# A three-layer feature-interaction kernel: the first pair of blocks read from two half tables

## The chip, the cores and the metric

The kernel runs on one core of a Trainium2 chip, in float32. The metric is the device time of a launch in microseconds (us); the time before is 734.22 us, the median of 3 runs (733.21 to 736.08). "Profile" and "trace" mean the record of one further execution by the hardware profiler. The engines are TensorE (PE, matrix multiplication; PEld is its weight load), VectorE (DVE), ScalarE (ACT), GpSimd (POOL) and SyncE (SP). GpSimd, ScalarE and SyncE issue transfers (DMA).

## What is computed

A batch of 1024 rows x has 39 fields of 64 numbers each. Three layers multiply every field of the layer's input with every field of x and mix the products by weights; each layer's output is summed over the 64 numbers, and a last row of weights makes one number per batch row:

```python
def _cin_layer(Xk, X0, W, b):
    O = W.shape[0]
    Hk, Fdim = (Xk.shape[1], X0.shape[1])
    Wr = W.reshape(O, Hk, Fdim)
    return jnp.einsum('bhe,bfe,ohf->boe', Xk, X0, Wr) + b[None, :, None]
X0 = sparse_embedding
Xk = X0
outs = []
for W, b in ((W0, b0), (W1, b1), (W2, b2)):
    Xk = _cin_layer(Xk, X0, W, b)
    outs.append(Xk.sum(axis=-1))
cin_output = jnp.concatenate(outs, axis=-1)
return cin_output @ fc_w.T + fc_b
```

Only sums of the second and third layer are wanted, so the kernel folds their weights with the last row (`v2` and its products), and the big work is one multiplication by 128 columns of weights: 64 for the first layer's output and 64 for the folded rest. It runs over the products of two fields; a product of fields a and b and that of b and a are the same, so their weights are added first and each pair is multiplied once.

## The kernel before

**Blocks and steps.** The batch is cut into 32 blocks of 32 rows (`BLK` = 2048 columns, a column being one of 64 numbers of one row). A block's x lies in memory field by field, 39 rows of 2048 columns and a row of ones, in one of three tables `xd`; a table holds a pair of blocks, n and n + 1, in rows 0 to 39 and 40 to 79. From it five tiles r (128 partitions x 2048) are gathered, each a chosen list of 128 fields (`lists`, an index per partition), so that the products of six pairs of tiles (`PAIRS`: 0·1, 0·2, 3·1, 3·2, 0·4, 3·4) hold nearly every pair of fields. What is missing is in a seventh product, u·v, shared by a pair of blocks: u and v have 4 groups of 32 partitions, one for each half (1024 columns, `SUB`) of each of the two blocks.

**Order of a pair of blocks.** Steps (n, 0) to (n, 5), then (n, 6), the u·v step, then (n + 1, 0) to (n + 1, 5). In each step VectorE multiplies two r tiles into p (`product`, L219; u·v L221) and TensorE multiplies p by the weights `wa`, a quarter of 512 columns at a time, into four banks of a block (`multiply`, L559). The u·v step (`join`, L579 and L590) uses 32-row pieces of TensorE and writes the banks of both blocks. There are four buffers p, and VectorE is asked for step k + 4 when TensorE is told of step k. After a block's last step ScalarE and VectorE multiply the two halves of its result and sum over the 64 numbers (`finish`, L607, L609, L620), and ScalarE copies 39 fields (`fields`, L602). On VectorE `finish` of a block stands between the products that are four steps ahead: that of block 0 between (1, 3) and (1, 4).

**Gathers and loads.** GpSimd issues all gathers (`gather_rows`, L174) in program order: `roll(n)` makes the five r tiles of a block, `roll_small(n)` u and v of a pair. `load(n)` (L168) brings a block's x into its table; most are issued by SyncE, those of blocks 1, 4 and 5 by GpSimd. A gather waits for the load of its table, for the last reader of its tile, and for the eighth DMA of GpSimd before it, as eight semaphores go round. Waits are put in by the framework from what each instruction reads and writes; the order is that of the program, written by hand.

**The first pair.** To start early, block 0's x is loaded by ScalarE in two halves `xh` of 1024 columns, and tiles 0 to 3 are gathered from these by halves (L389 to L394), with `load(1)` between. SyncE copies both halves into table 0 (L396), since tile 4 of block 0 (it needs the row of ones), u and v, and block 1's tiles are gathered from that table. During this TensorE folds the weights (L406 to L487), and VectorE adds weights for each step (`weight_rows`, L526), which TensorE transposes (`weight_turn`, L543). `spin` (L279) multiplies ones, to no use but keeping TensorE going. The loop at L689 to L730 then runs the steps; a step's `product` of number 5 of a block is followed by the `roll` of the block two later.

Of the kernel before, what the change touches and what calls it, by code (L numbers as in the profile page):

```python
# [62 lines left out]
FT = F + 1  # L63
# [84 lines left out]
def cin_kernel(ctx: ExitStack, tc: tile.TileContext, x, w0t, b0, w1, b1, w2, b2, fc_w, fc_b, out):  # L148
# [9 lines left out]

    xv = x.rearrange("b f e -> f b e")
    xd = [dram.tile([2 * FT, BLK], F32, name=f"xd{k}") for k in range(NTAB)]  # L160
    xh = [dram.tile([F, SUB], F32, name=f"xh{k}") for k in range(2)]

    def bank(name):
        return psum.tile([128, MM], F32, name=name, tag="po")
# [1 line left out]
    def load(n, engine=nc.sync):  # L166
        first = n % 2 * FT
        engine.dma_start(  # L168
            xd[n // 2 % NTAB][first : first + F].rearrange("f (b e) -> f b e", e=E),
            xv[:, n * BB : (n + 1) * BB, :],  # L170
        )

    def gather_rows(dst, table, k):
        nc.gpsimd.indirect_dma_start(  # L174
            dst, None, table, bass.IndirectOffsetOnAxis(ap=lists[:, k : k + 1], axis=0)
        )

    def roll(n, tiles=range(NT)):
        for i in tiles:
            k = n % 2 * NT + i  # L180
            gather_rows(rt[n % 2][:, i], xd[n // 2 % NTAB][: FT if k < NT else 2 * FT], k)

    def roll_small(n):
        table = xd[n // 2 % NTAB].rearrange("f (t c) -> (f t) c", c=SUB)
        for k, dst in enumerate((ut, vt)):
            gather_rows(dst[n // 2 % 2], table, 2 * NT + k)

    wa = const.tile([128, NCHUNK, 3 * H], F32, name="wa")
    columns = const.tile([128, 3], F32, name="columns")
# [8 lines left out]
    wfin = const.tile([H + F, 1], F32, name="wfin")  # L198
    kfin = const.tile([NY * 32, 1], F32, name="kfin")

    lists = const.tile([128, 2 * NT + 2], I32, name="lists")
# [23 lines left out]
    with prep as prep:  # L225
# [24 lines left out]
        nc.sync.dma_start(fcrow, fc_w)  # L250
        def load_half(k):
            nc.scalar.dma_start(
                xh[k].rearrange("f (b e) -> b f e", e=E), x[k * SB : (k + 1) * SB]
            )

        nc.scalar.dma_start(w2s, w2.rearrange("o (s n) -> (o s) n", s=2))
# [30 lines left out]
        spin()  # L287


        tmp = prep.tile([128, 16], F32, name="tmp")  # L290
# [77 lines left out]
        def fill_ones(k, engine, src):  # L368
            engine.dma_start(xd[k][F::FT].rearrange("r (p c) -> p r c", c=128), src)

        fill_ones(0, nc.gpsimd, ones)


        nc.vector.tensor_scalar(unit, apart, 0, None, ALU.is_equal)
        for h in (0, H):
# [4 lines left out]
        r, most, seat, far = (new() for _ in range(4))  # L380
# [6 lines left out]
        nc.vector.tensor_scalar(most, r, 23.0, 2.0, ALU.min, ALU.mult)  # L387

        halves = [slice(0, SUB), slice(SUB, BLK)]  # L389
        for k, cols in enumerate(halves):  # L390
            for i in range(4):
                gather_rows(rt[0][:, i, cols], xh[k], i)
                if k and i == 1:
                    load(1, nc.gpsimd)  # L394
        for k in (1, 0):
            nc.sync.dma_start(xd[0][0:F, halves[k]], xh[k])  # L396
        roll(0, (4,))

# [29 lines left out]
            )  # L428
        nc.vector.tensor_tensor(steps_at, steps_at, steps_by, ALU.mult)
        fused(seat, row, 96.0, seat, ALU.is_ge, ALU.add)  # L430
        step(row, 64.0, 2.0 * FT - 1.0, far)
        nc.vector.tensor_reduce(jumps, steps_at, AX.X, ALU.add)
        fused(most, r, 4.0, most, ALU.add, ALU.add)
        column = blocks.rearrange("h k (f j) -> h (k f) j", j=32)[:, :, 0]
# [26 lines left out]
        for k, n in enumerate((8, 5)):  # L461
            for t in range(2):
# [104 lines left out]
    def join(n, p):  # L567
        open_block(n + 1)

        def tiles(t, side):  # L570
            rows = slice(SQUARE * t, SQUARE * t + SQUARE)
            return rows, po[n + t // 2][2 * t % 4 + side]

        for side in range(2):
            for t in range(4):
                for half in range(2):
                    rows, dst = tiles(t, side)
                    at = (side + half) * H
                    nc.tensor.matmul(  # L579
                        dst[half * H : half * H + H],  # L580
                        wa[rows, NPAIR, at : at + H],
                        p[rows, bass.ts(side, MM)],
                        start=t >= 2,
                        stop=t < 2 and half == side,
                    )
        for t in range(4):
            for side in range(2):
                rows, dst = tiles(t, side)
                half = (1 - side) * H
                nc.tensor.matmul(  # L590
                    dst[half : half + H],
                    wa[rows, NPAIR + 1, H : 2 * H],
                    ut[n // 2 % 2][rows, bass.ts(side, MM)],
                    start=False,
                    stop=t < 2,
                )

    def fields(n):
# [88 lines left out]
        multiply(n, c, p[n, c], (1,))  # L687

    for at, (n, c) in enumerate(steps[:-TAIL]):  # L689
        if c == 0 and 2 <= n and n + 4 < NBLK:  # L690
            load(n + 4)
        quarters = range(BLK // MM)
        if at < 3:
            quarters = quarters[2:]
        if at < NPAIR and at > 1:
            multiply(n, c, p[n, c], quarters[:1])
            weight_turn(steps[at + 1][1])
            quarters = quarters[1:]
            if at == NPAIR - 1:
                multiply(n, c, p[n, c], quarters[:2])  # L700
                weight_turn(NPAIR + 1)
                quarters = quarters[2:]
        if c == NPAIR:
            join(n, p.pop((n, c)))
        else:
            multiply(n, c, p.pop((n, c)), quarters)
        if not at:
            fields(0)
            nc.scalar.copy(ones1, ones)
            fill_ones(1, nc.sync, ones1)  # L710
            for k in (2, 3):
                load(k)
        if at == NPAIR - 2:
            weight_rows(NPAIR + 1)
            for k in (NPAIR, NPAIR + 1):
                spread(k)
        if at - 1 in over:
            finish(over[at - 1])
            fields(over[at - 1] + 1)
        if at + AHEAD < len(steps):  # L720
            n, c = steps[at + AHEAD]
            if at + AHEAD <= NPAIR:
# [83 lines left out]
```

## Time and profile before

| | |
|---|---|
| time, median of 3 runs | 734.22 us (733.21 to 736.08) |
| time of the profiled execution | 733.14 us |
| its span, first to last instruction | 731.4 us |
| TensorE busy | 724.7 us, 99% of the span |
| VectorE busy | 638.3 us, 87% |
| GpSimd busy | 397.6 us, 54% |
| chain that ended last | TensorE 99% |
| L559, 128x512 multiplications | 1536 records, mean 594 ns |
| L219, products | 198, mean 2224 ns |
| L174, gathers into r from the tables `xd` | 156, mean 1938 ns |
| L174, gathers into r from the halves `xh` | 8, mean 996 ns |
| bytes moved by DMA | 197.24 MB, mean 270 GB/s |

Busy time is the share of the span in which an engine executes; overlapping instructions count once. A line of a timeline reads: start in us from the span's start, us taken, engine, line, operation, output tile and inputs, number of instructions merged into it, and in brackets the idle time of that engine before it and what ended it. A line of the chain reads: start, us, engine, output, line. In the lines on stretches, after the stretch and the busy times stand TensorE's granted clock, DMA's busy share and GB/s. One 32-bit multiplication shows as two records.

### The profile page before, as it was taken

What the parts mean: (1) busy time and instruction counts of PE and PEld (TensorE: products, weight loads), DVE (VectorE), ACT (ScalarE), POOL (GpSimd) and SP (SyncE); (2) the same over time, 40 slices, a digit from 0 to 9 for tenths busy, and PEclk for the clock granted to TensorE, in tenths of its full rate; (3) what the DMA queues carried; (4) which work ended last, traced back from release to release, by engine and by line L of the source; (5) the groups of instructions that cost most, each with busy time, mean ns of one, the idle gap of its engine ahead of it and who ended that gap; (6) DMA issues with size and microseconds to landing.
All of it is one profiled execution on the core that took longest, in us unless ns stands there. A gap on an engine that the chain in (4) does not pass through costs nothing.

```text
span 731.4 us, 6351 instructions
## 1 busy us (share of the span) xinstructions
PE 724.7 (99%) x2375; PEld 316.1 (43%) x2375; DVE 638.3 (87%) x521; ACT 166.9 (23%) x240; POOL 397.6 (54%) x254
## 2 busy tenths in 40 slices
PE   8999999999999999999999999999999999999998
PEld 4444444444444444444444444444444444444443
DVE  6999798988889988889988889888898988889885
ACT  3332121222212222221222212222121221212222
POOL 6789886536555445754537555455654547545300
PEclk9999999999999999999999999999999999999999
DMA  8997899789575887757679675896767777565700
GB/s 268 376 337 280 315 342 356 290 307 338 232 273 231 281 336 286 270 225 285 269 288 330 223 289 219 304 348 236 268 256 274 301 287 266 224 252 236 288 0 0
DMA packets 65983, 197.24 MB, mean 270 GB/s; under 512 B 40110, under 2 KB 40179, under 8 KB 45984
## 3 DMA queue, kind: packets, MB, share of 16 engines
q0 software_dynamic: 28784, 185.56, 65.5%
q1 hardware_dynamic: 35468, 9.29, 5.5%
q10 hardware_dynamic: 1700, 1.99, 1.0%
q8 instruction: 18, 0.29, 0.1%
q14 instruction: 13, 0.11, 0.0%
HBM read 196.76 MB, written 10.60 MB: 284 GB/s over the span
## 4 chain that ended last, share of the span: by engine, by line
PE 99%; DVE 0%; DMA 0%; issue 0%; ACT 0%; DVEq 0%
PE po L559 91%; PE po L579 4%; PE po L590 2%; PE idle L279 0%; PE pv L406 0%; PE pt L487 0%; PE small L323 0%; PE pv L487 0%; PE pw L418 0%; DMA fcrow<-in_fc_w 0%; PE tr L543 0%; DVE g L609 0%; DVE pairs L526 0%; DVE sums L631 0%; ACT z L607 0%
## 5 line engine op out<-in xcount | busy, mean ns | idle before, releaser
L559 PE MATMUL po<-p,wa 128*128 128x512 f32 x1536 | 666.0, 594 | 0.0
L219 DVE TENSOR_TENSOR p<-r 128x2048 f32<-128x2048 f32 (+2 forms) x198 | 434.1, 2224 | 72.4 <-PE po L559 67.1
L559 PEld LDWEIGHTS po<-p,wa 128*128 128x128 f32 x1536 | 290.5, 190 | 371.7 <-issue 354.6
L174 POOL DMA_INDIRECT r<-xd,lists x156 | 302.3, 1938 | 267.1 <-issue 266.2
L607 ACT ACTIVATE z<-po,columns 64x512 f32<-64x512 f32 x128 | 87.3, 682 | 380.1 <-PE po L590 217.9
L609 DVE SCALAR_TENSOR_TENSOR g<-po,b0s,z 64x512 f32<-64x512 f32 x128 | 95.9, 749 | 9.3 <-ACT z L607 5.3
L602 ACT COPY g<-r 39x1024 f32<-39x1024 f32 x64 | 66.7, 1043 | 155.0 <-DVE sums L620 126.8
L620 DVE TENSOR_REDUCE sums<-g 103x16 f32<-103x1024 f32 x62 | 75.6, 1220 | 2.1
L174 POOL DMA_INDIRECT u<-xd,lists x16 | 38.9, 2432 | 7.5 <-issue 4.6
L174 POOL DMA_INDIRECT v<-xd,lists x16 | 38.5, 2403 | 4.9 <-issue 4.9
L579 PE MATMUL po<-p,wa 32*64 32x512 f32 x512 | 31.6, 600 | 0.0
L221 DVE TENSOR_TENSOR p<-u,v 128x1024 f32<-128x1024 f32 x16 | 19.5, 1218 | 0.0
L579 PEld LDWEIGHTS po<-p,wa 32*64 32x64 f32 x512 | 9.4, 131 | 20.2 <-issue 19.4
L590 PE MATMUL po<-u,wa 32*64 32x512 f32 x256 | 17.0, 587 | 0.0
L174 POOL DMA_INDIRECT r<-xh,lists x8 | 8.0, 996 | 4.8 <-DVE tmp L387 2.7
L590 PEld LDWEIGHTS po<-u,wa 32*64 32x64 f32 x256 | 5.7, 132 | 8.0 <-issue 8.0
L526 DVE TENSOR_TENSOR pairs<-both 128x2 f32<-128x2 f32 (+27 forms) x59 | 6.1, 171 | 0.2
L544 ACT COPY wa<-tr 128x128 f32<-128x128 f32 x8 | 2.1, 266 | 16.2 <-PE tr L543 16.2
L279 PE MATMUL idle<-const-float32-1.0 128*128 128x256 f32 (+1 forms) x8 | 4.0, 596 | 0.8 <-PEq L793 0.8
L543 PE MATMUL tr<-unit,pairs 128*128 128x128 f32 x8 | 2.4, 294 | 2.2 <-DVE pairs L526 2.2
L543 PEld LDWEIGHTS tr<-unit,pairs 128*128 128x128 f32 x8 | 1.2, 151 | 4.7 <-ACT pairs L524 2.7
L168 POOL DMA_DIRECT2D xd<-in_x x3 | 3.2, 1055 | 0.0
(97 smaller groups left out, 56.7 us busy)
## 6 DMA issues: line engine op xcount, KB each, us to landing
xd<-in_x SPq DMA_DIRECT2D x28, 312.0 KB
r<-xd,lists POOLq DMA_INDIRECT x156, 8.9
xd<-in_x POOLq DMA_DIRECT2D x3, 312.0 KB, 7.6
w2s<-in_w ACTq DMA_DIRECT2D x1, 624.0 KB
w1s<-in_w ACTq DMA_DIRECT2D x1, 624.0 KB
w0s<-in_w0t ACTq DMA_DIRECT2D x1, 380.2 KB
xh<-in_x ACTq DMA_DIRECT2D x2, 156.0 KB
xd<-xh SPq DMA_DIRECT2D x2, 156.0 KB
```

The lines of the kernel that those rows point to most:

```text
L174: nc.gpsimd.indirect_dma_start(dst, None, table, bass.IndirectOffsetOnAxis(ap=lists[:, k : k + 1], axis=0))
L219: nc.vector.tensor_tensor(p[:, cols], r[:, i, cols], r[:, k, cols], ALU.mult)
L221: nc.vector.tensor_tensor(p[:, 0:SUB], ut[n // 2 % 2], vt[n // 2 % 2], ALU.mult)
L279: nc.tensor.matmul(idle[:, 0:cols], nc.const_aps.tensor(1.0, (128, 128), F32), nc.const_aps.tensor(1.0, (128, cols), F32), start=True, sto ...
L526: nc.vector.tensor_tensor(out, diagonal(a, b, sa, sb), diagonal(b, a, sb, sa), ALU.add)
L559: nc.tensor.matmul(po[n][m], wa[:, c, side : side + 2 * H], p[:, bass.ts(m, MM)], start=n % 2 == 0 and c == 0, stop=n % 2 == 1 and c == NP ...
L579: nc.tensor.matmul(dst[half * H : half * H + H], wa[rows, NPAIR, at : at + H], p[rows, bass.ts(side, MM)], start=t >= 2, stop=t < 2 and ha ...
L590: nc.tensor.matmul(dst[half : half + H], wa[rows, NPAIR + 1, H : 2 * H], ut[n // 2 % 2][rows, bass.ts(side, MM)], start=False, stop=t < 2,)
L602: nc.scalar.copy(gt[H : H + F], rt[n % 2][0:F, 0, bass.ts(m, SUB)])
L607: nc.scalar.activation(z[one], po[n][m][other], AF.Identity, bias=fc0s[other])
L609: return lambda: nc.vector.scalar_tensor_tensor(g[n][m // 2][0:H, at], po[n][m][one], b0s[one], z[one], ALU.add, ALU.mult)
L620: nc.vector.tensor_reduce(sums[:, b_at : b_at + SB], g[n][m // 2].rearrange("p (b e) -> p b e", e=E), AX.X, ALU.add,)
```

## The change

- The halves `xh` become tables of 80 rows each, like `xd` but with 1024 columns: rows 0 to 38 block 0's x, row 39 ones, rows 40 to 78 block 1's x, row 79 ones. The ones are written by two DMAs of GpSimd.
- All gathers of the first pair read these: tiles 0 to 3 of block 0 as before, tile 4 in two halves, u and v in two halves of 64 partitions each, block 1's five tiles in two halves each.
- SyncE's copies into table 0 are dropped. Block 1's x is loaded in two halves by GpSimd, after the eight gathers of tiles 0 to 3 instead of between them.
- The groups of u and v change places, so that the first 64 partitions belong to the first half of the columns; `seat`, `far` and `lists` follow (two more columns of `lists` for the halves), and so do the banks in `join`.
- Table 0 is first used for block 6; its row of ones is written later. The loads of blocks 6 and 7 are issued by GpSimd instead of SyncE.
- The name of the change also speaks of no filling on TensorE between T and the first turn. The diff has no such edit: the calls of `spin` are the same in both kernels.

```diff
-    xh = [dram.tile([F, SUB], F32, name=f"xh{k}") for k in range(2)]
+    xh = [dram.tile([2 * FT, SUB], F32, name=f"xh{k}") for k in range(2)]
...
     def gather_rows(dst, table, k):
+        at = lists[0 : dst.shape[0], k : k + 1]
         nc.gpsimd.indirect_dma_start(
-            dst, None, table, bass.IndirectOffsetOnAxis(ap=lists[:, k : k + 1], axis=0)
+            dst, None, table, bass.IndirectOffsetOnAxis(ap=at, axis=0)
+        )
+
+    def roll_half(n, i, h):
+        k = n * NT + i
+        rows = F if n == 0 and i < NT - 1 else (n + 1) * FT
+        gather_rows(rt[n][:, i, bass.ts(h, SUB)], xh[h][0:rows], k)
...
     def roll_small(n):
-        table = xd[n // 2 % NTAB].rearrange("f (t c) -> (f t) c", c=SUB)
         for k, dst in enumerate((ut, vt)):
-            gather_rows(dst[n // 2 % 2], table, 2 * NT + k)
+            if n:
+                table = xd[n // 2 % NTAB].rearrange("f (t c) -> (f t) c", c=SUB)
+                gather_rows(dst[n // 2 % 2], table, 2 * NT + k)
+            else:
+                for h in range(2):
+                    gather_rows(dst[0][h * H : h * H + H], xh[h], 2 * NT + 2 + k)
...
-        fill_ones(0, nc.gpsimd, ones)
-
+        for k in range(2):
+            nc.gpsimd.dma_start(
+                xh[k][F::FT].rearrange("r (p c) -> p r c", c=128), ones[0:8]
+            )
...
-        for k, cols in enumerate(halves):
-            for i in range(4):
-                gather_rows(rt[0][:, i, cols], xh[k], i)
-                if k and i == 1:
-                    load(1, nc.gpsimd)
-        for k in (1, 0):
-            nc.sync.dma_start(xd[0][0:F, halves[k]], xh[k])
-        roll(0, (4,))
+        for at in range(8):
+            roll_half(0, at % 4, at // 4)
+        for k in range(2):
+            nc.gpsimd.dma_start(
+                xh[k][FT : FT + F].rearrange("f (b e) -> f b e", e=E),
+                xv[:, BB + k * SB : BB + (k + 1) * SB, :],
+            )
+        for k in range(2):
+            roll_half(0, 4, k)
...
-        step(row, 64.0, 2.0 * FT - 1.0, far)
+        step(row, 64.0, 1.0 - 2.0 * FT, far)
...
-        nc.vector.tensor_tensor(seat, seat, far, ALU.add)
+        nc.vector.tensor_scalar(half_seat, seat, float(FT), None, ALU.mult)
+        fused(seat, seat, 2.0 * FT, far, ALU.mult, ALU.add)
...
-        nc.vector.tensor_scalar(lists[:, 2 * NT :], both_of, 2.0, seat, ALU.mult, ALU.add)
+        nc.vector.tensor_scalar(lists[:, 2 * NT + 2 :], both_of, half_seat, None, ALU.add)
+        nc.vector.tensor_scalar(
+            lists[:, 2 * NT : 2 * NT + 2], both_of, 2.0, seat, ALU.mult, ALU.add
+        )
         roll_small(0)
-        roll(1)
+        for i in range(NT):
+            for k in range(2):
+                roll_half(1, i, k)
...
-        fill_ones(2, nc.gpsimd, ones)
+        for k in (2, 0):
+            fill_ones(k, nc.gpsimd, ones)
...
-            return rows, po[n + t // 2][2 * t % 4 + side]
+            return rows, po[n + t % 2][t // 2 * 2 + side]
...
-        if c == 0 and 2 <= n and n + 4 < NBLK:
+        if c == 0 and 4 <= n and n + 4 < NBLK:
             load(n + 4)
...
-                if n < 2:
+                if n < 4:
                     load(n + 4, nc.gpsimd)
```

More of the change, by code (lines that the diff above doesn't have):

```diff
@@ L199, in cin_kernel @@
     kfin = const.tile([NY * 32, 1], F32, name="kfin")
-    lists = const.tile([128, 2 * NT + 2], I32, name="lists")
+    lists = const.tile([128, 2 * NT + 4], I32, name="lists")
     rt = [const.tile([128, NT, BLK], F32, name=f"r{k}") for k in range(2)]
@@ L252, in load_half @@
             nc.scalar.dma_start(
-                xh[k].rearrange("f (b e) -> b f e", e=E), x[k * SB : (k + 1) * SB]
+                xh[k][0:F].rearrange("f (b e) -> b f e", e=E), x[k * SB : (k + 1) * SB]
             )
@@ L287, in cin_kernel @@
         spin()
-        tmp = prep.tile([128, 16], F32, name="tmp")
+        tmp = prep.tile([128, 18], F32, name="tmp")
         wide = prep.tile([128, 5, NT], F32, name="wide")
@@ L379, in cin_kernel @@
             )
-        r, most, seat, far = (new() for _ in range(4))
+        r, most, seat, far, half_seat = (new() for _ in range(5))
         both_of = prep.tile([128, 2], F32, name="both_of")
@@ L582, in join @@
                         p[rows, bass.ts(side, MM)],
-                        start=t >= 2,
-                        stop=t < 2 and half == side,
+                        start=t % 2 == 1,
+                        stop=t % 2 == 0 and half == side,
                     )
@@ L594, in join @@
                     start=False,
-                    stop=t < 2,
+                    stop=t % 2 == 0,
                 )
```

## The prediction

> **What bounds the kernel now.** I read first the chain of work that ended last. After its first rows it is TensorE alone:
>
> ```profile
> 16.43 0.30 PE tr L543
> ...
> 40.30 1.90 PE po L579 x32
> 42.20 0.86 PE po L590 x16
> 43.06 41.40 PE po L559 x96
> 84.46 1.90 PE po L579 x32
> ```
>
> Each next piece starts where the last one ends: from the first real multiplication (17.14 us) to 726 us TensorE doesn't pause, and of the 731.4 us span only about 17 at the front and 5 at the end are anything else. So the change can shorten only the front. Anything late after 17 us lengthens the kernel by what exceeds its slack, and such a loss is not won back, as TensorE has no spare time. Need times, from this view: the last u·v step (L579) at 40.30; block 1's first product at 43.06; then one step each 41.40/12 = 3.45 us.
>
> Next, what feeds TensorE: the timelines of VectorE and of GpSimd from 14 us on. VectorE:
>
> ```profile
> 20.31 2.35 DVE L219 TENSOR_TENSOR p<-r 128x1024 f32<-128x1024 f32 x2
> 23.38 2.50 DVE L219 TENSOR_TENSOR p<-r 128x1024 f32<-128x1024 f32 x2 [0.72 <-DMA r<-xh,lists]
> ...
> 26.78 2.35 DVE L219 TENSOR_TENSOR p<-r 128x1024 f32<-128x1024 f32 x2
> ...
> 29.77 2.28 DVE L219 TENSOR_TENSOR p<-r 128x2048 f32<-128x2048 f32 x1
> ...
> 37.22 2.29 DVE L219 TENSOR_TENSOR p<-r 128x2048 f32<-128x2048 f32 x1 [0.39 <-DMA r<-xd,lists]
> ...
> 52.35 11.09 DVE L219 TENSOR_TENSOR p<-r 128x2048 f32<-128x2048 f32 x5
> ```
>
> GpSimd, whose gathers fill r, u and v:
>
> ```profile
> 18.65 1.66 POOL L174 DMA_INDIRECT r<-xd,lists  x1 [0.30 <-issue]
> 23.23 0.94 POOL L174 DMA_INDIRECT u<-xd,lists  x1 [2.92 <-DVE p L219]
> 24.47 0.95 POOL L174 DMA_INDIRECT v<-xd,lists  x1 [0.30 <-issue]
> 25.73 0.96 POOL L174 DMA_INDIRECT r<-xd,lists  x1 [0.30 <-issue]
> 27.00 3.09 POOL L174 DMA_INDIRECT r<-xd,lists  x1 [0.30 <-issue]
> 30.39 2.61 POOL L174 DMA_INDIRECT r<-xd,lists  x1 [0.31 <-issue]
> 33.30 2.70 POOL L174 DMA_INDIRECT r<-xd,lists  x1 [0.30 <-issue]
> ...
> 51.80 12.45 POOL L174 DMA_INDIRECT u<-xd,lists  x1 [0.30 <-issue]
> ```
>
> The same instruction takes 0.94 us or 12.45. Lay the two lists over each other: the gather of 27.00 ends at 30.09, 0.95 after the products of 26.78 end (29.13); that of 30.39 ends at 33.00, 0.95 after the product of 29.77 (32.05); that of 51.80 at 64.25, 0.8 after five products in a row (63.44). A gather that meets running products gets in when the row of products breaks. The three of 23.23 to 26.7 were quick because VectorE waited there for a landing (0.72) and then made small weight sums. So between 26.7 and 36 one gather passed per break, about one in 3 us. Product (1,0) (block 1, pair 0) ran 37.22 to 39.51: slack to 43.06 is 3.55 us.
>
> **What the Trainium skill says.** "SBUF — State Buffer", section "Who interferes with whom": VectorE and GpSimd share a port pair under an exclusive lock; a VectorE instruction with two SBUF inputs contends with a GpSimd instruction that reads SBUF, and the later one blocks fully. A gather reads its `lists` in SBUF, a product reads two tiles: the trace agrees (12.45 against 0.94 us). "A bandwidth-pool intuition that's wrong" there puts the release at about 115 ns after VectorE's end; here 0.8 to 0.95, nearly a whole gather. "DMA: Bandwidth & Descriptors", "Anatomy of one DMA", prices a transfer at 2.0 us + bytes/436 GB/s, so 3.2 us for 512 KB; the trace has 4.6 at the least from a gather's start, 3.7 from its end. "TensorE: Matmul & The Clock Gate", Part 1: an idle window of about 3.4 us halves TensorE's clock. The stretches agree: 1.00 in 14 to 16 us, 0.50 in 18 to 20 after the pause of 14.3 to 16.4.
>
> **The change part by part.**
>
> *Front to 17 us: 0.* Two more VectorE index instructions (0.15 to 0.25 us each by their neighbours) at 9.4 to 10.3 lie in the 1.55 us of idle time before 11.66; uncovered they would cost 0.4. A second ones DMA on GpSimd (0.64 to 0.76) lies in its 2.71 us idle before 7.17. TensorE's list is unchanged here: no filling is added or removed, whatever the change's name says.
>
> *Copies gone, block 1's load moved behind the eight gathers: gain on VectorE, 0 on TensorE.* 312 KB of copy and 312 KB of load leave the path of tiles 2 and 3's second halves; at 0.39 MB/us (stretch 18 to 22) that is 0.8 to 1.6 us, more than VectorE's wait of 0.72, which goes. TensorE didn't wait for it. But that wait was the door through which u passed. Now four products stand in one row from 20.3 to 25.0.
>
> *Twice the gathers.* Tile 4: 2 for 1. u, v: 4 for 2. Block 1's r: 10 for 5. GpSimd cost alone 8 x (0.94 + 0.30) = 9.9 us; the half gathers (937 to 1246 ns) show that half the bytes costs no less. What matters is doors. Walk of GpSimd's queue, start + 0.94, or 0.8 after a blocking row:
> - Tiles 2 and 3 end 17.0; two half loads of 1.06: 19.1; tile 4's first half 19.4 to 20.4, its second is caught by the row: 25.0 + 0.8 = 25.8, lands about 29; product (0,4) runs about 29 to 31.3, needed at 33.1: hidden.
> - u's first half is caught by (0,3)'s two products (26 to 28.3): 29.1. u's second by (0,4): 32.0. v's first by (0,5) (32 to 34.3): 35.1. v's second is free: 36.4, lands 38.7 to 40. u·v product 1.21: 40 to 41, needed at 40.3: 0 to 0.7 late.
> - Block 1's tiles 0 and 1: four halves at 1.25, one caught by the u·v product: 42.0, landing 45.0 to 45.7. Product 2.29: 47.3 to 48.0 against 43.06: **4.3 us late** (4.3 to 4.9).
> - Then (1,1), (1,2), (1,3) follow landings to about 55.6; the end of block 0 on VectorE (46.84 to 52.35 before: 5.5 us) stands ahead of (1,4): 61.1 + 2.3 = 63.4; TensorE wants it at 47.4 + 4 x 3.45 = 61.2: **2.3 us late**.
> - Block 2's gathers started at 43.13; now ten gathers, five small loads and one more ones DMA stand ahead, until about 61, then (1,4) and (1,5) catch the first. Product (2,0), wanted at about 70, is **0 to 5 late**; I take 1.
> - Half clock after the 4 us pause: 3.4/2 = 1.7, largely absorbed by the later waits, since a slow TensorE waits less; I take 1.2.
>
> Sum 4.3 + 2.3 + 1 + 1.2 = 8.8.
>
> *Remaining edits: 0.* The new order of halves in `join` has the same 24 multiplications on as many banks; banks of block n+1 are touched two instructions earlier, some 17 us after they were freed. Loads of blocks 6 and 7 move from SyncE to GpSimd: 2 x 1.06 us, 40 us ahead of use; without that lead they would be one landing late (7.6).
>
> The profiled execution took 733.14 us (span 731.4); with 8.8 it is 741.9. The median of the runs is 1.1 above it: 734.2 + 8.8 = **743.0**.
>
> **Rivals.** *Gathers pass anyway (not slower).* If GpSimd gets in where one product ends and the next begins, the queue runs at 1.25 us each: block 1's fourth half is issued by about 33 and lands by 37 to 38, as before. For: the gather of 43.13 ends at 45.60, inside two products in a row (42.42, 4.50), so that did happen once. Against: 51.80 passed no such seam in 11 us. It decides if that half lands by 43.06 - 2.3 = 40.7. Time 734 (733 to 736).
>
> *One door more.* A single seam or a late landing near 22.6 lets one gather through early: all moves by 1.2 to 3 us, the first loss is 1.5 to 3, the second shrinks: 736 to 739.5.
>
> *Tile 4 caught twice.* If its first half misses 20.3, its second ends at 29.0 and lands at 32: (0,4) ends 34.3 against 33.1, and the rest shifts: 745 to 749.
>
> *Faster.* Fewer bytes (312 KB of copies) and no wait on VectorE would shorten a kernel bound by transfers. DMA is full from 16 to 44 us here, but TensorE doesn't wait for it. What is left is a lucky phase of the clock window at 17 to 20 us: 732 to 733.
>
> **How the numbers follow.** Main case (739.5 to 745) 0.55, tile 4 caught twice 0.12, one door more 0.17, gathers pass 0.14, faster 0.02. Change under 0.5% (3.7 us), about what a measurement of this kernel can tell, holds "gathers pass" and a quarter of "one door more": same 0.18, slower 0.80, faster 0.02. The range 735 to 749 leaves out most of "gathers pass", "faster" and a tail above; the likeliest case alone is 739.5 to 745.
>
> **What would show it.** TensorE idle time before L559 on VectorE's product near 43 and 61 us; its chain with VectorE and DMA pieces there. The 0.72 us wait at 22.7 gone. A gather beginning near 20.7 and lasting about 5 us; u and v ending near 29, 32, 35 and 36. Block 2's first gather at about 60 instead of 43.13. A clock below 1.00 after about 47. I am wrong if half gathers stay near 0.94 us while products run, or if TensorE's chain is unbroken after 17 us.

## The result, and the profile after

The changed kernel takes 741.28 us (median of 6 runs, 739.45 to 742.38) against 734.32 us for the kernel before on the same chip (6 runs, 733.21 to 736.08): the ratio is 1.0091, with a 95% interval of 1.0074 to 1.0107. It is slower by 7.0 us. The profiled execution took 740.66 us with a span of 738.9 us (before: 733.14 and 731.4), so the two traces differ by 7.5 us.

What TensorE waited for, in the changed kernel (engine, output and line that waited, who released it: us in all, times, longest):

```profile
PE po L579 <- DVE p L229: 3.0, 1, 3.0
PE tr L563 <- DVE pairs L546: 2.3, 1, 2.3
PE po L599 <- DVE p L231: 1.9, 1, 1.9
```

The middle line is the pause before the first turn (TensorE's first transposition of summed weights), which the kernel before has too (2.2 us). The first and the third are new: once TensorE waited for a product of r tiles, once for the u·v product. The chain that ended last shows where, and whom it leads back to:

```profile
25.65 2.95 POOL u L175
28.90 2.60 POOL v L175
31.81 2.69 POOL v L175
34.81 0.94 POOL r L175
...
38.55 6.23 DMA r<-xh,lists
44.90 2.31 DVE p L229
47.25 44.11 PE po L579 x96
91.36 1.90 PE po L599 x32
```

In the kernel before this chain was TensorE alone from 17 us on. Now it goes through GpSimd's gathers of u, v and block 1's first tiles, the landing of the fourth half tile (gather begun at 38.55), and VectorE's product (1,0). TensorE starts on block 1 at 47.25, where it did so at 43.06 before, and then needs 44.11 us for the 96 records of blocks 1 and 2 (twelve steps) instead of 41.40. GpSimd's timeline:

```profile
21.63 1.24 POOL L175 DMA_INDIRECT r<-xh,lists  x1 [0.30 <-issue]
24.43 0.92 POOL L175 DMA_INDIRECT u<-xh,lists  x1 [1.55 <-DVE p L229]
25.65 2.95 POOL L175 DMA_INDIRECT u<-xh,lists  x1 [0.30 <-issue]
28.90 2.60 POOL L175 DMA_INDIRECT v<-xh,lists  x1 [0.30 <-issue]
31.81 2.69 POOL L175 DMA_INDIRECT v<-xh,lists  x1 [0.31 <-issue]
...
38.55 0.94 POOL L175 DMA_INDIRECT r<-xh,lists  x1 [0.31 <-issue]
...
55.77 1.00 POOL L175 DMA_INDIRECT r<-xd,lists  x1 [1.36 <-issue]
```

and VectorE's:

```profile
20.78 3.65 DVE L229 TENSOR_TENSOR p<-r 128x1024 f32<-128x1024 f32 x3 [1.25 <-DMA r<-xh,lists]
...
25.33 2.35 DVE L229 TENSOR_TENSOR p<-r 128x1024 f32<-128x1024 f32 x2
...
28.31 2.28 DVE L229 TENSOR_TENSOR p<-r 128x2048 f32<-128x2048 f32 x1
...
31.44 2.28 DVE L229 TENSOR_TENSOR p<-r 128x2048 f32<-128x2048 f32 x1
...
39.14 1.23 DVE L231 TENSOR_TENSOR p<-u,v 128x1024 f32<-128x1024 f32 x1 [4.89 <-issue]
44.90 2.29 DVE L229 TENSOR_TENSOR p<-r 128x2048 f32<-128x2048 f32 x1 [4.53 <-DMA r<-xh,lists]
```

Laid over each other: the three gathers of 2.6 to 2.95 us each end 0.8 to 0.9 us after a product of VectorE ends (25.33 + 2.35 = 27.68, and 28.60; 30.59, and 31.50; 33.72, and 34.50). Three slow gathers between 25 and 35 us, as in the kernel before; but there they were block 1's tiles, and here they are the second half of u and both halves of v. Block 1's gathers begin at 34.81 instead of 25.73.

What that does to the transfers is seen in the stretch from 30 to 36 us (after the stretch: busy us of PE, PEld, DVE, ACT, POOL, then TensorE's clock, DMA's busy share, GB/s), before:

```profile
30.00:36.00 6.00, 6.00 (x16) 2.68 (x16) 6.00 (x20) 1.57 (x12) 5.39 (x3) 1.00 1.07 398
```

and after:

```profile
30.00:36.00 6.00, 6.00 (x17) 2.69 (x16) 4.25 (x19) 1.88 (x13) 5.14 (x3) 1.00 0.38 113
```

GpSimd is as busy as before, with three gathers in both. Those of v now ask for a quarter of the bytes (64 partitions x 1024 for 128 x 2048) and that of r for half, and the DMA engines run at 113 GB/s instead of 398.

The 7.5 us, piece by piece along TensorE: the first multiplication starts 2.04 us earlier (15.10 against 17.14); from there to the join 2.16 more, 1.87 of it the wait for the u·v product; from the join's start to (1,0) 4.07 more, 2.98 of it the wait for the product; then 2.71 more for the multiplications of blocks 1 and 2, of which the first ran at half clock:

```profile
46.00:48.00 2.00, 0.75 (x1) 0.50 (x2) 1.76 (x2) 1.01 (x2) 2.00 (x1) 0.50 1.02 416
```

In the kernel before the clock was 1.00 in this stretch. After these blocks 0.6 us is lost in all. In the join 1.0 us (L610 took 2.08 us instead of 1.06) has no wait beside it in the trace, and is not explained.

### The profile page after: what moved, and what is told of

Same layout as the page of the kernel before. It is cut to its first block, busy times and chain, and to the rows that moved or that the text cites. A ratio compares the mean times of both kernels' runs of the same rounds, so it can differ in the third digit from the quotient of the medians.

```text
span 738.9 us, 6363 instructions
## 1 busy us (share of the span) xinstructions
PE 727.0 (98%) x2375; PEld 315.7 (43%) x2375; DVE 638.9 (86%) x523; ACT 166.8 (23%) x240; POOL 409.8 (55%) x267
## 4 chain that ended last, share of the span: by engine, by line
PE 93%; POOL 2%; DMA 2%; DVE 1%; issue 1%; ACT 0%; DVEq 0%
PE po L579 87%; PE po L599 4%; DMA r<-xh,lists 2%; PE po L610 2%; POOL r L175 1%; DVE p L229 1%; POOL v L175 1%; POOL u L175 1%; PE small L333 0%; DVE g L629 0%; DVE sums L651 0%; ACT z L627 0%; POOL shifts L325 0%; DVE twice L389 0%; DVE fc L370 0%
## 5 line engine op out<-in xcount | busy, mean ns | idle before, releaser
L175 POOL DMA_INDIRECT r<-xd,lists x150 | 311.4, 2076 | 260.1 <-issue 255.1
L175 POOL DMA_INDIRECT r<-xh,lists x20 | 24.3, 1216 | 7.7 <-issue 5.8
L175 POOL DMA_INDIRECT v<-xd,lists x15 | 25.6, 1706 | 4.6 <-issue 4.6
L175 POOL DMA_INDIRECT u<-xd,lists x15 | 25.5, 1699 | 4.6 <-issue 4.0
L610 PE MATMUL po<-u,wa 32*64 32x512 f32 x256 | 18.4, 587 | 0.0
L610 PEld LDWEIGHTS po<-u,wa 32*64 32x64 f32 x256 | 6.2, 132 | 8.9 <-issue 8.9
L175 POOL DMA_INDIRECT v<-xh,lists x2 | 5.3, 2648 | 0.6 <-issue 0.6
L175 POOL DMA_INDIRECT u<-xh,lists x2 | 3.9, 1934 | 1.9 <-DVE p L229 1.6
```

The lines of the kernel that those rows point to most:

```text
L175: nc.gpsimd.indirect_dma_start(dst, None, table, bass.IndirectOffsetOnAxis(ap=at, axis=0))
L610: nc.tensor.matmul(dst[half : half + H], wa[rows, NPAIR + 1, H : 2 * H], ut[n // 2 % 2][rows, bass.ts(side, MM)], start=False, stop=t % 2 ...
```

## Experiments

Each time is a median in us, with the kernel before on the same chip beside it.

| run | time | before | ratio (95% interval) |
|---|---|---|---|
| the change | 741.28 | 734.32 | 1.0091 (1.0074 to 1.0107) |
| before, small edits alone | 733.25 | 733.24 | 1.0005 (0.9993 to 1.0017) |
| before, gathers doubled alone | 741.51 | 733.89 | 1.0098 (1.0069 to 1.0128) |
| change, u and v not doubled | 740.22 | 733.24 | 1.0094 (1.0073 to 1.0116) |
| the same, block 1's r whole, one load more | 738.97 | 733.24 | 1.0061 (1.0041 to 1.0081) |
| change, breaks between products | 736.74 | 733.89 | 1.0033 (1.0022 to 1.0045) |
| change, pause filled | 741.18 | 733.89 | 1.0096 (1.0064 to 1.0128) |
| change, nothing doubled but tile 4 | 736.66 | 733.89 | 1.0039 (1.0027 to 1.0051) |
| the same, loads of blocks 6, 7 late | 737.65 | 733.82 | 1.0047 (1.0030 to 1.0064) |
| the same, and breaks | 733.46 | 734.19 | 0.9991 (0.9979 to 1.0002) |
| the same, breaks and filling | 733.62 | 734.19 | 0.9990 (0.9981 to 0.9999) |
| late loads and filling, no breaks | 737.69 | 733.82 | 1.0056 (1.0039 to 1.0073) |
| before, filling alone | 733.69 | 733.82 | 1.0003 (0.9994 to 1.0012) |

The theory under test, the lock theory: a gather can't run while VectorE's products run in a row, so what counts is how many gathers stand ahead of block 1's tiles for how many breaks, a break being a point where the row of products ends. Its rivals: the loss lies in the half tables and missing copies themselves, in bytes and landings, in the moved loads, or in TensorE's clock.

### One part alone

The small edits on the kernel before:

```diff
-            return rows, po[n + t // 2][2 * t % 4 + side]
+            return rows, po[n + t % 2][t // 2 * 2 + side]
...
-                        start=t >= 2,
+                        start=t % 2 == 1,
...
-        if c == 0 and 2 <= n and n + 4 < NBLK:
+        if c == 0 and 4 <= n and n + 4 < NBLK:
...
-                if n < 2:
+                if n < 4:
                     load(n + 4, nc.gpsimd)
```

> The kernel before with only the small edits of the change: the new seating of u and v (still one gather each from the whole table), the new order of halves in the join, loads of blocks 6 and 7 issued by GpSimd. Lock theory (the loss comes from the doubled gathers): no change, 734.3 us (733 to 736), and TensorE without a pause after its first multiplication. Rival (the new order in the join or the moved loads cost something): 736 or more, with the 0.37 us by which the second pair's join grew, and about 1 us more inside the first join.

They cost nothing (1.0005). Their trace has one thing more to tell: there the first multiplication began at 15.68 us instead of 17.14, and TensorE then waited 0.57, 0.26 and 0.55 us for VectorE, so the join began at 40.97, later than the 40.30 of the kernel before. In this trace an early front was given back, because VectorE waited for the landings of the tiles' second halves (0.77, 1.29 and 1.08 us).

Then the doubled gathers alone, from the whole table:

```diff
+            if not n:
+                for h in range(2):
+                    gather_part(
+                        dst[0][h * H : h * H + H], table, lists[0:H, 2 * NT + 2 * h + k :][:, 0:1]
+                    )
+                continue
...
-        roll(1)
+        for i in range(NT):
+            for h in range(2):
+                gather_rows(
+                    rt[1][:, i, bass.ts(h, SUB)],
+                    xd[0].rearrange("f (t c) -> (f t) c", c=SUB),
+                    2 * NT + 4 + h * NT + i,
+                )
```

> The kernel before with only the number of gathers doubled: u and v in two halves of 64 partitions each, block 1's r in ten half tiles instead of five, all from the whole table; copies, loads and the order of everything else as before (three small index instructions more on VectorE, in the idle time of the front). Lock theory: block 1's first two halves take the breaks that its first two tiles took, its fourth half is issued at about 38 to 39 instead of 33, and product (1,0) ends at 45 to 47 instead of 39.5, against 43.06: 4.5 to 8 us above the kernel before. Rival (the half tables, the missing copies or the later load of block 1 cause the loss): within 1 us of the kernel before.

741.51 us: the whole loss of the change, with the copies and the old loads, and with half tables only for block 0's tiles 0 to 3, as in the kernel before. GpSimd's timeline of this run:

```profile
26.73 3.10 POOL L177 DMA_INDIRECT v<-xd,lists  x1 [0.30 <-issue]
30.13 2.66 POOL L177 DMA_INDIRECT r<-xd,lists  x1 [0.31 <-issue]
33.09 2.69 POOL L177 DMA_INDIRECT r<-xd,lists  x1 [0.30 <-DVE pairs L550]
...
37.74 0.94 POOL L177 DMA_INDIRECT r<-xd,lists  x1 [0.30 <-issue]
```

The breaks near 30, 33 and 36 us let one gather through each, as before; the fourth half of block 1 goes out at 37.74 (38 to 39 was expected). TensorE began (1,0) at 46.83 after a wait of 4.00:

```profile
46.83 43.38 PE L583 MATMUL po<-p,wa 128*128 128x512 f32 x96 [4.00 <-DVE p L226]
```

So doubling is enough for the whole loss. That it is also needed for it is not said by this run.

### Fewer gathers in the change

Both half tables in one table, so that u and v take one gather each:

```diff
-                for h in range(2):
-                    gather_rows(dst[0][h * H : h * H + H], xh[h], 2 * NT + 2 + k)
+                gather_rows(dst[0], xs, 2 * NT + 2 + k)
```

> The changed kernel with both half tables in one table of DRAM, so that u and v take one gather each again (two gathers fewer, everything else as changed; two or three small index instructions more on VectorE at the front). Lock theory: two doors of about 3 us come free, so the u.v product is on time, block 1's fourth half is issued at about 37 instead of 39.5, and product (1,0) ends at about 44.5 instead of 47.2: 738.5 us (736.5 to 739.5). If the loss were in bytes or landings, which are the same, 741 as the changed kernel.

No gain in time that the intervals show: 740.22 us, ratio 1.0094 beside 1.0091. The trace shows why two gathers fewer bring little:

```profile
25.84 2.78 POOL L176 DMA_INDIRECT u<-xs,lists  x1 [2.16 <-DVE pairs L549]
28.93 0.94 POOL L176 DMA_INDIRECT v<-xs,lists  x1 [0.30 <-issue]
30.18 2.43 POOL L176 DMA_INDIRECT r<-xs,lists  x1 [0.30 <-issue]
32.91 2.81 POOL L176 DMA_INDIRECT r<-xs,lists  x1 [0.30 <-issue]
...
37.67 0.94 POOL L176 DMA_INDIRECT r<-xs,lists  x1 [0.30 <-issue]
```

The u·v product came at 35.35 instead of 39.14, and its wait in the join is gone. But u started 1.4 us later than in the trace of the change, its one gather was caught, and block 1's first halves were caught in the places that v had. The fourth half went out at 37.67 instead of 38.55: 0.9 us won, where 2.5 were expected.

Then block 1's r in five whole gathers as well, from a table of its own that an additional load fills:

```diff
+        nc.gpsimd.dma_start(
+            xb[0:F].rearrange("f (b e) -> f b e", e=E), xv[:, BB : 2 * BB, :]
+        )
...
         for i in range(NT):
-            for k in range(2):
-                roll_half(1, i, k)
+            gather_rows(rt[1][:, i], xb, i)
```

> As the run with one table, and block 1's r in five whole gathers again, from a whole table of block 1 that one more load of 312 KB fills. Number of gathers behind tile 4 as before the change, bytes more than in either kernel. Lock theory: block 1's second tile is issued by about 34.5 to 35.8, lands by 41, product (1,0) ends by 43.3 at the latest: 734.5 us (733 to 736.5). If bytes set the loss: above 741.

738.97 us, 0.6% above the kernel before and not level with it (the ten runs lie between 734.58 and 740.85). Its GpSimd:

```profile
20.45 5.25 POOL L177 DMA_INDIRECT r<-xs,lists  x1 [0.30 <-issue]
25.70 1.06 POOL L412 DMA_DIRECT2D xb<-in_x  x1
...
33.92 2.21 POOL L177 DMA_INDIRECT r<-xb,lists  x1 [3.73 <-issue]
```

The second gather of tile 4 met four products in a row and took 5.25 us, so the load behind it went out at 25.70 and block 1's first gather only after its landing, at 33.92. The number of gathers was as before, and block 1 was late all the same. I had only counted gathers; here one long row of products did the harm, through the additional load that it held back.

### Breaks

If rows of products are what holds the gathers, it must help to break them. A memset that reads nothing, before each product of block 0 in the changed kernel, and the two whole products in halves:

```diff
+    door = const.tile([128, 96], F32, name="door")
...
+        if n == 0 and c in (4, 5) and cols == slice(0, BLK):
+            for h in range(2):
+                product(n, c, slice(h * SUB, h * SUB + SUB), p)
+            return p
+        if n == 0 and c < NPAIR:
+            nc.vector.memset(door, 0.0)
```

> The changed kernel with breaks between VectorE's products of block 0: a memset of 128x96, which reads nothing, before each of them, and the two whole products (0,4) and (0,5) each in two halves. Lock theory, if a break this short lets a waiting gather in: u's second half and both halves of v end about 1.2 us earlier each, block 1's fourth half is issued at about 36 to 37 instead of 39.5, time 2 to 4 us below the changed kernel (ratio to before 1.004 to 1.007). If a gather needs a longer break, no change (1.009) or a little slower. Byte theory: no change.

736.74 us, ratio 1.0033: some two thirds of the loss is gone, with all fourteen gathers of u, v and block 1's r still there and VectorE's list longer. GpSimd's timeline:

```profile
25.66 0.90 POOL L175 DMA_INDIRECT u<-xh,lists  x1 [0.30 <-issue]
26.86 1.85 POOL L175 DMA_INDIRECT v<-xh,lists  x1 [0.30 <-issue]
29.02 0.89 POOL L175 DMA_INDIRECT v<-xh,lists  x1 [0.30 <-issue]
30.21 1.62 POOL L175 DMA_INDIRECT r<-xh,lists  x1 [0.30 <-issue]
...
35.45 0.94 POOL L175 DMA_INDIRECT r<-xh,lists  x1 [0.30 <-issue]
```

A caught gather costs 1.6 to 1.85 us instead of 2.6 to 2.95, and the next one passes in 0.9. Half the gathers are free. The fourth half goes out at 35.45 instead of 38.55, and (1,0) starts at 43.38 right behind the join. TensorE's timeline then shows the next loss:

```profile
43.38 14.16 PE L587 MATMUL po<-p,wa 128*128 128x512 f32 x32
60.32 29.43 PE L587 MATMUL po<-p,wa 128*128 128x512 f32 x64 [2.78 <-DVE p L237]
```

32 records are four steps, so the 2.78 us stand before (1,4): the end of block 0 on VectorE (52.47 to 58.0) lies between (1,3) and (1,4), and the product follows it only at 57.98, half a microsecond after TensorE asks for it. The profiled execution took 738.70 us, 2.0 more than the median, so this wait may be larger than in most.

### The clock after the pause

Three multiplications by zeros in the pause, to keep the clock full:

```diff
         if c == NPAIR:
             join(n, p.pop((n, c)))
+            if n == 0:
+                for _ in range(3):
+                    nc.tensor.matmul(
+                        po[1][0],
+                        nc.const_aps.tensor(0.0, (128, 128), F32),
+                        nc.const_aps.tensor(1.0, (128, MM), F32),
+                        start=False,
+                        stop=False,
+                    )
```

> The changed kernel with three multiplications by a weight of zeros between the first join and product (1,0), about 2.6 us of TensorE work in the pause of 3 us, so that the clock isn't halved after it. If the half clock is a loss of its own: 2.7 us below the changed kernel (ratio to before about 1.0055). If a faster TensorE only waits for (1,1) to (1,4) instead, as the record of VectorE suggests ((1,4) ends 0.7 us before it is wanted): about 0.7 us below (1.008).

741.18 us, as the change. TensorE's timeline of this run:

```profile
47.35 14.00 PE L579 MATMUL po<-p,wa 128*128 128x512 f32 x32 [1.63 <-DVE p L229]
62.58 27.73 PE L579 MATMUL po<-p,wa 128*128 128x512 f32 x64 [1.23 <-DVE p L229]
...
108.69 27.73 PE L579 MATMUL po<-p,wa 128*128 128x512 f32 x64 [1.68 <-DVE p L229]
```

At full clock four steps take 14.00 us, and TensorE waits 1.23 us before (1,4) and 1.68 before (3,4), which it didn't in the change. The next join began at 90.24 us, 1.05 earlier than in the trace of the change (91.29), and the wait before (3,4) took that back. So the half clock (2.7 us) is no loss of its own: without it TensorE waits for VectorE instead. With four runs the interval is wide (1.0064 to 1.0128); it leaves out a gain of 2.7 us, but not one of the 0.7 us that was the other answer.

### The change without its doubled gathers

Block 0's halves and block 1's whole rows in one table; no copies, one load of block 1 behind the eight gathers; u, v and block 1's r one gather each (tile 4 stays in two):

```diff
+    xs = dram.tile([4 * FT, SUB], F32, name="xs")
+    xw = xs.rearrange("(f t) c -> f (t c)", t=2)
...
+            if n == 1:
+                gather_rows(rt[1][:, i], xw, k)
+                continue
...
+            if not n:
+                gather_rows(dst[0], xs, 2 * NT + 2 + k)
+                continue
```

> The change without its doubled gathers: the half tables of block 0 and the whole table of block 1 lie in one table of DRAM; no copies, block 1 loaded once, after the eight gathers of the front; tile 4 in two halves as in the change, but u and v one gather each and block 1's r five. Lock theory: nothing after the front is late; what the change took out of the front (312 KB of copies, the load in the middle of the gathers) shows alone: 0 to 2 us below the kernel before (ratio 0.997 to 1.000). If the half tables themselves or the missing copies cost: still 1.005 or more.

736.66 us, 0.4% above before; it should have been level. The profiled execution took 734.49 us, the second fastest of 17, and in it tile 4's second half got through in 1.85 us. I put the rest on SyncE: with the first table of x out of use, nothing held back its loads of blocks 6 and 7. The next run moves these behind their step, as the change does:

```diff
-        if c == 0 and 2 <= n and n + 4 < NBLK:
+        if c == 0 and 4 <= n and n + 4 < NBLK:
...
-                if n < 2:
+                if n < 4:
```

> The run without doubled gathers, with one more part of the change: the loads of blocks 6 and 7 come from GpSimd behind their step instead of from SyncE. In the run without them SyncE issued four loads at 22.6 to 31.0, where both kernels issue two: the first table of x was no longer in use, so nothing held the loads of blocks 6 and 7 back, and their 624 KB stood before block 1's tiles in DMA engines that were full. If that is why product (1,0) waited 2.15 us and a later product 0.94: no wait after the first multiplication, 731 to 733.5 us, ratio to before 0.996 to 0.9995. If the half tables or the single table cost in themselves: 1.004 again.

737.65 us: that guess was wrong too. VectorE's timeline of this run

```profile
20.30 4.62 DVE L226 TENSOR_TENSOR p<-r 128x1024 f32<-128x1024 f32 x4
```

beside GpSimd's

```profile
20.64 5.23 POOL L175 DMA_INDIRECT r<-xs,lists  x1 [0.31 <-issue]
26.18 2.95 POOL L175 DMA_INDIRECT u<-xs,lists  x1 [0.30 <-DVE pairs L543]
```

and the stretch from 22 to 26 us

```profile
22.00:26.00 4.00, 4.00 (x11) 1.73 (x10) 4.00 (x15) 2.87 (x7) 3.87 (x1) 1.00 0.39 148
```

give another cause: four products in one row, one gather of 5.23 us behind them, and DMA engines at 148 GB/s (the kernel before has 408 there). If it is the row, breaks must remove all that is left:

```diff
+        if n == 0 and c in (4, 5) and cols == slice(0, BLK):
+            for h in range(2):
+                product(n, c, slice(h * SUB, h * SUB + SUB), p)
+            return p
+        if n == 0 and c < NPAIR:
+            nc.vector.memset(door, 0.0)
```

> The run with late loads (no doubled gathers), with the breaks between VectorE's products of block 0. In the run without breaks four products stood in one row from 20.3 to 24.9, since VectorE no longer waits for a landing there; the gather behind it took 5.2 us and the DMA engines moved next to nothing from 24 to 26 us. If this lockout is what is left of the loss, tile 4, u, v and block 1's first two tiles go out 2 to 5 us earlier, product (1,0) is on time, and the time is that of the kernel before or up to 2 us less: ratio 0.997 to 1.001. If the table itself or the transfers cost it: 1.004 to 1.005 again.

733.46 us, ratio 0.9991: the loss is gone, by breaks alone. Tile 4's second half, u and v pass:

```profile
19.42 0.96 POOL L175 DMA_INDIRECT r<-xs,lists  x1 [0.30 <-issue]
23.83 1.01 POOL L175 DMA_INDIRECT u<-xs,lists  x1 [3.45 <-DVE door L230]
25.15 0.94 POOL L175 DMA_INDIRECT v<-xs,lists  x1 [0.30 <-issue]
```

and TensorE has no pause between the first multiplication and block 1's end. One wait is left, later, which the kernel before doesn't have:

```profile
102.42 27.73 PE L584 MATMUL po<-p,wa 128*128 128x512 f32 x64 [1.23 <-DVE p L234]
```

It stands before (3,4), in an execution of 734.91 us, 1.5 above the median, and no run takes it away. In the time, block 0's half tables and the missing copies leave no cost once the rows are broken; what they bring is at most 0.2%, the lower end of the interval. Block 1's tiles, u and v take one gather each here, so this doesn't speak for the doubled gathers of the change.

### Filling before the first turn

Four small multiplications of constants where TensorE waits about 2 us for the first turn of weights, in three kernels:

```diff
         for k, a in groups:
             nc.tensor.matmul(
...
+        spin(4)
```

> The kernel before with the same four multiplications of constants between the last fold multiplication and the first turn, and nothing else. Same three answers: up to 1.7 us below before if the clock is what counts (ratio 0.9977), within 0.7 us if landings limit the front (0.999 to 1.000; a trace of the kernel before with small edits, whose front was 1.5 us earlier, gave 1.4 us of it back in waits), 1.3 us above if the filling runs at half clock.

> As the run with late loads, with four small multiplications of constants (1.7 us at full clock) on TensorE between the last fold multiplication and the first turn, where TensorE waits 2.0 to 2.3 us. If the clock is then not halved at the first products, up to 1.7 us below the run with late loads; if the landings of the tiles' second halves limit the front, as the waits on VectorE before the third and fourth product suggest (1.25 us), less than 0.7 us. If the filling itself runs at half clock (3.4 us), the first turn is late by 1.3 us: that much above.

> The same with the four multiplications of constants between the folds and the first turn. The trace with late loads and this filling had the clock full throughout and no pause before the first turn, but 1.07 us of waiting for the first turned weight; the kernel before with this filling was unchanged in time. So 0 to 1 us below the run without it: ratio 0.996 to 1.000.

In the traces of all three the clock is full from the first multiplication on. The time doesn't follow: 1.0003 on the kernel before; 1.0056 beside 1.0047 with late loads; 0.9990 beside 0.9991 with breaks. All three differences lie within the intervals; with breaks and filling the change is level with the kernel before or 0.1% below it. In the last two the waits for VectorE stay: with breaks and filling TensorE still waits 0.52 us before (1,4) and 1.36 before (3,4).

## Why the prediction was right, and where it wasn't

The forecast was 743.0 us and slower; measured were 741.28 us and slower, within the likeliest case (739.5 to 745). The mechanism, one gather for each break, is what the runs show. That the number came so near is in part luck: two errors behind (1,0) cancelled, and the terms after it were added although they hide each other.

**What bounds it: right.** From the first multiplication on only lateness counted, and it wasn't won back: nearly all of the loss lies before 92 us of the span.

**Front 0: right for the change, though not in the traces.** The first multiplication began 2.04 us earlier after the change. Nothing in TensorE's list differs there, but its fold multiplications took less time. Before:

```profile
10.33 2.36 PE L487 MATMUL pt<-w1s,v 128*128 128x320 f32 x4
```

After:

```profile
9.57 1.39 PE L507 MATMUL pt<-w1s,v 128*128 128x320 f32 x4
```

In the other runs this start lies between 15.7 and 16.8 us with the front of before, and between 14.6 and 17.8 with fronts of the change. It goes with the execution and not with the kernel. Why the folds take 2.36 or 1.39 us is not shown: the view of the clock has 1.00 for both from 9 to 13 us.

**Copies gone and four products in one row: the mechanism was right, the profiled run missed it.** I said that VectorE's wait at 22.7 us was the door through which u passed, and that without it a gather of about 5 us would stand from 20.7. The trace of the change shows VectorE still waiting (1.25 us before 20.78), and tile 4's second half through in 1.24 us. But four runs built on the change show that gather: 19.86 for 4.59 us, 20.29 for 5.23, 20.45 for 5.25 and 20.64 for 5.23. Whether it comes goes with the start: in the three traces with the change's front and without breaks where TensorE's first multiplication began by 15.10 us VectorE waited, in the four where it began at 16.00 or later it didn't. With nothing doubled but tile 4, breaks brought 1.0047 to 0.9991, some 4 us; they open all rows of block 0, so this is the price of all the rows and not of this one.

**Twice the gathers: right in pattern, near in number by luck.** u's and v's halves ended at 25.35, 28.60, 31.50 and 34.50; forecast were 29.1, 32.0, 35.1 and 36.4. They were earlier than the walk since tile 4 wasn't caught, but in the same pattern of one gather for each break, until the last half of v, which was caught too. Product (1,0) began at 44.90 (forecast 45.0), TensorE at 47.25 (forecast 47.3 to 48.0). But the fourth half tile's gather ended at 39.49, 2.5 us before the walk's 42.0, and landed 5.3 us later (38.55 + 6.23 = 44.78), where the walk gave it 3.0 to 3.7. I had taken about the least landing of the trace before (4.6 us from a gather's start); the median there is 8.9 (L174). So the queue was that of my rival "one door more", for which I forecast 736 to 739.5 us, and a landing that I had too short made up for it. The u·v product was 1.87 us late against a front that had come 2 us early: the join began at 40.42, 0.1 later than before; forecast were 0 to 0.7.

**The terms behind (1,0): this step failed.** I added 2.3 us for (1,4), 1 for (2,0) and 1.2 for the half clock, 4.5 in all. Measured were 2.71, all as half clock, and nothing at (1,4) and (2,0). The half clock itself was sized too small: I took one window of 3.4 us, but the stretches have 0.50 from about 45.8 to 52.6, 6.8 us, and 5.4 of these had work. (A pause of 3.0 us stood before it, and one of 2.2 us before the 0.50 of the kernel before; both are shorter than the idle window of 3.4 us in the prediction.) And the terms can't be added, as one hides the other: product (1,4) was ready at 63.0 (forecast 63.4), and TensorE, slowed by the half clock, loaded weights for it at 63.30 without a pause; with the pause filled it came earlier and waited 1.23 us, then 1.68 before (3,4), and the time was the same. The run with breaks, whose clock was full up to there, waited 2.78 us. With 2.3 alone the sum would have been 4.3 + 2.3 = 6.6, and the time 740.8 us; that is hindsight, and the loss that came was the other term. Block 2's first gather came at 55.77, not at about 60, and (2,0) wasn't late.

**Remaining edits 0: right** (1.0005 for the new seats, the join's order and the moved loads).

**The Trainium skill.** "SBUF — State Buffer", section "Who interferes with whom", on the exclusive lock carried the forecast, and the gathers beside the products agree (up to 5.25 us in block 0). Two things in the traces go beyond it: the section has the lock held for an instruction, while a gather here waited through rows of four, and small weight sums with two inputs in SBUF let gathers through. In the section "A bandwidth-pool intuition that's wrong" the release comes about 115 ns after VectorE's end. The 0.8 to 0.9 us here, and the 0.8 to 0.95 that I set against it in the prediction, run to the end of the gather, of which a free gather is 0.94; they don't measure the release and don't contradict the page.

**What went wrong after the prediction.** Four expectations missed. Three times (one table, block 1's r whole, nothing doubled but tile 4) I counted gathers and not rows of products, and once I blamed SyncE's loads. Only breaking the rows told these apart. Breaks on the kernel before were not tried; as its TensorE has no wait for a product, I would expect nothing from them.

## What to carry to other kernels

Where GpSimd's gathers and VectorE's two-input products share the time, as in this kernel, count the breaks in VectorE's list and the gathers that stand for them; a gather's bytes matter less than its place in that queue. A wait of VectorE for a landing can be such a break, and an edit that removes the wait closes it; a memset of 128x96 between the products opened it again here for some 0.04 us of VectorE. When several things are late one behind the other, ask first which hides which, and don't add them; and take landings at their usual length in a full queue and not at their least.

## What the runs showed of the hardware that I had not expected

- A memset of 128x96 (0.14 us in the record, overlapping its neighbours; products then start 1.19 us apart instead of 1.15) lets a waiting gather in, while the seam between two products in a row mostly doesn't: 5.23 us behind four products without it, 0.9 to 1.85 us with it. Whether it is because the memset reads nothing was not tested. One seam did let a gather in: in the kernel before that of 43.13 ended at 45.60, 0.9 us after the first of two products in a row (42.42 + 2.29 = 44.71), and the traces of the small edits and of the filling alone have it too. What makes that seam different is not shown.
- Small weight sums of VectorE let gathers in as well. They too have two inputs in SBUF, but 11 of them take 1.08 us: in the run with breaks the gather of 25.66 took 0.90 us beside them (25.68 to 26.76). So what opens the lock may be that an instruction is short; no run tells.
- While a gather is locked out, the DMA engines run dry: 18 GB/s in the stretch from 24 to 26 us of the run with late loads, against 383 in the kernel before. Nothing new is asked for meanwhile; that what was asked for earlier has been moved by then is a reading of that figure, and not a test.
